# The experts' second layer by seven products of quarters, its input sums on GpSimd, the combination two experts behind

## The chip, the cores and the metric

The kernel runs on one core of one Trainium2 chip. The metric is the device time of one execution in microseconds (us), taken as the median over several executions. A core has five engines that work side by side, each through its own queue in order: TensorE (PE, with its weight loads shown apart as PEld), VectorE (DVE), ScalarE (ACT), GpSimd (POOL) and SyncE (SP, which here issues the DMAs).[...]

## The reference

Two stages run over 4096 tokens of 256 numbers (32 x 128 tokens), all in float32. Layer 0 is an attention block. Layer 1 is a windowed attention (24 tokens wide), followed by a mixture of eight experts, each with three dense layers:

```python
t = _to_tokens(x)                                    # after layer 0
t = t + _L1_attn_ref(_ln_t(t), K, temperature, bias) # window of 24 tokens
t = t + _L1_ffn_ref(_ln_t(t), ...)

def _L1_ffn_ref(x, Wr, br, W1, b1, ..., W2, b2, ..., Wo, bo):
    feat = jnp.mean(x, axis=0)
    w = jax.nn.softmax(feat @ Wr + br, axis=-1)      # weights of the 8 experts
    h = jnp.einsum('bfd,edh->bfeh', x, W1) + b1      # first layer,  256 -> 256
    h = jax.nn.relu(_bn(h, g1, be1, m1, v1))
    h = jnp.einsum('bfeh,ehk->bfek', h, W2) + b2     # second layer, 256 -> 256
    h = jax.nn.relu(_bn(h, g2, be2, m2, v2))
    y = jnp.einsum('bfeh,ehd->bfed', h, Wo) + bo     # third layer,  256 -> 256
    return jnp.einsum('bfed,fe->bfd', y, w)          # combination of the experts
```

The batch is one, so the mean over it changes nothing and every token has its own eight weights.

## The kernel before

The first 760 us or so are layer 0, which the change doesn't touch. The rest is one function in which windowed attention and experts run interleaved. Tokens lie in 32 tiles of 128, four tiles make a group (`TPB` = 4, so a block of `BLK` = 512 tokens), and there are eight groups (`NGRP`). For each group and each of the eight experts there is one work item, 64 in all.

The order on PE, ACT, DVE and POOL is written out by hand. Time is cut into slots. A slot first issues the attention steps that are due in it, those on other engines than PE first (the names in `POSTS`), then those on PE, and then one piece of expert work (`piece`). An engine takes its instructions exactly in this order. A work item has three pieces, a group 24 slots (`PERIOD` = 3 * 8). A slot number below is meant modulo 24, counted from the group's own first slot.

Attention steps of a group, with their slots: `project_out` (PE, 0 and 1), `residual` (DVE: an addition and the statistics of two tiles, 1 and 2; it also starts the load of a later pair, whose addition is on POOL), `root` (ACT, 3), `centre` (DVE, 4), `turn` and `turned` (PE and ACT, 5 to 7), `keys_tile` (POOL, 7), `project` and `projected` (PE and ACT, 8 to 10), `logits`, `rectified`, `weighed`, `windowed` (PE, DVE, ACT, DVE, 11 to 15), `gather` (PE, 15 and 17), `gathered` (DVE, 16 and 18: two tiles each time), `root` (ACT, 20). Then the experts' input is made: `expert_input` (DVE, 21), `expert_turn` (PE, 22), `expert_turned` (ACT, 23), `expert_sums` (DVE, 24), which writes four sums of quarters of the input. Then come the routing weights (`route` to `route_norm`, slots 26 to 31, that is 2 to 7 of the next group), `bias_sum` (POOL, in four slots from 32 on: the biases `bo` weighted and summed over the experts) and `biased` (DVE, 50, that is slot 2 two groups later: two additions).

Expert work. The first layer is a product of a 256 x 256 matrix with a 256 x 512 block. It is computed by Winograd's form of Strassen's method: both are cut into quarters, and seven products of a 128 x 128 quarter with 128 x 256 replace eight. `open_first` makes four of the products into two PSUM tiles `pa` and `pb`. DVE then reads them in four steps (lines 1825 to 1828, called the chain of four below) into `u` and `c`. `close_first` adds three more products on top, which is why its first two, into `pb`, must wait until the chain of four has read `pb`. DVE then makes two quarters more (line 1846), and ACT applies scale, shift and ReLU in three instructions (line 1856). The second layer (`layer`, line 1867) is plain: four products of 128 x 128 with 128 x 512, and two ACT instructions (line 1875). `combine` (lines 1892 and 1901) is the third layer: in each half four products of 256 columns and two DVE instructions that add the weighted result to `h1`.

The three pieces of work item k before are:

```python
part 0:  open_first(k + 1);       combine(k - 1, first half)
part 1:  combine(k - 1, second half);  close_first(k + 1)
part 2:  layer(k)
```

A float32 product shows in the profile as two matmul records. The two bank rings that matter are `ps_h` (four PSUM tiles: `pa`, `pb` and the second layer's two) and `ps_y` (two, for `combine`).

Of the kernel before, what the change touches and what calls it, by code (L numbers as in the profile page):

```python
# [9 lines left out]
F32 = mybir.dt.float32  # L10
AF = mybir.ActivationFunctionType
# [4 lines left out]
P = 128  # L16
# [807 lines left out]
def short(ctx: ExitStack, tc: tile.TileContext, ins: dict, out: bass.AP, flag):  # L824
# [538 lines left out]
    NRING = 12  # L1363
    with ExitStack() as ff:
# [23 lines left out]
        A = wf.tile([P, E, 7, P], F32, name="A")  # L1388
        W = {}
        for name in ("W2", "Wo"):  # L1390
            W[name] = wf.tile([P, E, 2, D], F32, name=f"{name}_sb")
        for e in range(E):
            w1 = ins["L1_ffn_W1"][e].rearrange("(c p) (m k) -> p c m k", p=P, k=P)
            a21 = fx.tile([P, P], F32, tag="a21", name=f"a21_{e}")
            nc.sync.dma_start(out=A[:, e, 0:2, :], in_=w1[:, :, 0, :])
            nc.sync.dma_start(out=a21, in_=w1[:, 0, 1, :])
            nc.sync.dma_start(out=A[:, e, 2, :], in_=w1[:, 1, 1, :])
            s = A[:, e]
            nc.gpsimd.tensor_tensor(s[:, 3], a21, s[:, 2], op=ALU.add)
            nc.gpsimd.tensor_tensor(s[:, 4], s[:, 3], s[:, 0], op=ALU.subtract)  # L1400
            nc.gpsimd.tensor_tensor(s[:, 5], s[:, 0], a21, op=ALU.subtract)
            nc.gpsimd.tensor_tensor(s[:, 6], s[:, 1], s[:, 4], op=ALU.subtract)
            for name in ("W2", "Wo"):
                nc.sync.dma_start(
                    out=W[name][:, e],
                    in_=ins[f"L1_ffn_{name}"][e].rearrange("(c p) h -> p c h", p=P),
                )
# [85 lines left out]
        def keys_tile(g):  # L1493

            kt = fx.tile([P, 2, 6 * P], F32, tag="kt", name=f"kt{g}")
            if g:
                old, at = kts[g - 1]
                base = (TPB * g + 1) * P - EDGE
                nc.gpsimd.tensor_copy(
                    kt[:, :, : P + EDGE], old[:, :, base - at : base - at + P + EDGE]  # L1500
                )
                kts[g] = kt, base
            else:
                kts[g] = kt, 0
# [14 lines left out]
        def projected(g, q):  # L1519
            kt, base = kts[g]  # L1520
            ps = banks.pop(("k", q)).rearrange("p (m k) -> p m k", m=2)
            nc.scalar.copy(kt[:, :, 2 * q * P - base : 2 * (q + 1) * P - base], ps)
# [6 lines left out]
        def logits(g, js, early=False):  # L1529
            kt, base = kts[g]  # L1530
# [22 lines left out]
        def rectified(js):  # L1553
            ps = banks.pop(("s", js[0])).rearrange("p (r k) -> p r k", r=2)
            pt = fx.tile([P, 2, WQ], F32, tag="pw", name=f"pw{js[0]}", bufs=4)
# [56 lines left out]
        def expert_input(b):  # L1612
            lo, hi = b * TPB, (b + 1) * TPB
            nc.vector.reciprocal(rstd2[:, lo:hi], rstd2[:, lo:hi])
            xf = fx.tile([P, TPB, D], F32, tag="xf", name=f"xf{b}", bufs=1)
            for r in range(TPB):
                normalise(lo + r, mean2, rstd2, xf[:, r, :])
            blk[b] = [xf]

        def expert_turn(b, early=False):  # L1620
            (xf,) = blk[b]
            pt = [bank(f"ptf{b}_{c}", early) for c in range(2)]
            for r in range(TPB):
                for c in range(2):
                    nc.tensor.transpose(
                        pt[c][:, r * P : (r + 1) * P], xf[:, r, c * P : (c + 1) * P], ident
                    )
            banks["x", b] = pt

        def expert_turned(b):  # L1630
            xfT = big_t[:, :, b * BLK : (b + 1) * BLK]
            for c, ps in enumerate(banks.pop(("x", b))):
                nc.scalar.copy(xfT[:, c, :], ps)
            blk[b] = [xfT]
# [3 lines left out]
        def expert_sums(b):  # L1638

            v = blk[b][0].rearrange("p c (n k) -> p c n k", n=2)  # L1640
            t = fx.tile([P, 4, HB], F32, tag="ts", name=f"ts{b}")
# [55 lines left out]
        def bias_sum(b, r):  # L1697

            w = blk[b][1]
            if r == 0:  # L1700
                blk[b].append(fx.tile([P, TPB, D], F32, tag="wb", name=f"wb{b}", bufs=1))
            out = blk[b][2][:, r, :]
            for k in range(2):
                t = fx.tile([P, E // 2, D], F32, tag="wbe", name=f"wbe{b}_{r}_{k}", bufs=1)
                es = slice(k * E // 2, (k + 1) * E // 2)
                nc.gpsimd.tensor_tensor(  # L1706
                    t, bo[:, es], w[:, r, es].unsqueeze(2).to_broadcast([P, E // 2, D]),
                    op=ALU.mult,
                )
                nc.gpsimd.tensor_tensor(t[:, :2], t[:, :2], t[:, 2:], op=ALU.add)  # L1710
                if k:
                    nc.gpsimd.tensor_tensor(t[:, 0], t[:, 0], t[:, 1], op=ALU.add)
                    nc.gpsimd.tensor_tensor(out, out, t[:, 0], op=ALU.add)
                else:
                    nc.gpsimd.tensor_tensor(out, t[:, 0], t[:, 1], op=ALU.add)
# [25 lines left out]
        def group(g):  # L1741
# [3 lines left out]
            js = list(range(TPB * g + 1 if g else 0, min(TPB * g + 5, NTILE)))  # L1745
            return qs, [js[k : k + 2] for k in range(0, len(js), 2)]

        def steps(g):
# [30 lines left out]
            put(21, expert_input, g)  # L1779
            put(22, expert_turn, g)  # L1780
            put(23, expert_turned, g)
            put(24, expert_sums, g)
# [255 lines left out]
```

## Time and profile before

| | |
|---|---|
| device time, median of 3 (lowest to highest) | 1552.93 us (1551.06 to 1554.34) |
| span of the profiled execution | 1551.5 us |
| layer 0 and the first group's attention | up to about 794 us |
| the interleaved stretch | 794 to 1551.5 us |
| one work item with no attention step in it | 9.91 us from open to open |
| the eight work items of a middle group | 95.5 us |
| DVE, ACT, POOL busy in the interleaved stretch (757.6 us) | 395.1, 263.8, 290.6 us |

The last three rows are read from the timeline: the starts of the first product of `open_first` (line 1819, `psa<-big_t,A`) are 9.91 us apart where no attention is left, as near the end, and 10.8 to 13.4 us apart where attention steps lie between. A timeline row gives start, busy time, engine, line, operation, output and inputs, and in brackets how long the engine had been idle and what ended it.

### The profile page before, as it was taken

The numbers are of one execution on the slowest core, as the hardware profiler recorded it, in microseconds if no ns is written. First come the engines' busy times: TensorE is split into PE (matmuls) and PEld (weight loads), VectorE is DVE, ScalarE is ACT, GpSimd is POOL, SyncE is SP. The second block draws the span as 40 slices with busy tenths as digits, with TensorE's granted clock in tenths as the row PEclk, the third lists the DMA queues.
The fourth block names the chain that finished last, engine by engine and source line by source line (L and its number), as shares of the span: only waits on it lengthen the run. The fifth ranks groups of instructions, "written<-read, shape, count | busy, mean of one in ns | idle before, by whom it ended". The sixth has DMA issues, their size and how long they took to land.

```text
span 1551.5 us, 22383 instructions
## 1 busy us (share of the span) xinstructions
PE 1514.8 (98%) x8932; PEld 818.6 (53%) x8932; DVE 995.1 (64%) x1461; ACT 823.1 (53%) x1077; POOL 359.6 (23%) x487
## 2 busy tenths in 40 slices
PE   7999999999999999999779999999999999999998
PEld 5663332222222222222357776777777777777775
DVE  5543567789888988989854555545455464555553
ACT  3225778788888888888433333333333334333332
POOL 0001110000000000000328053180622706226080
PEclk9999999999999999999999999999999999999999
DMA  4200000000000000000430000000000000000000
GB/s 119 62 1 14 18 9 9 9 8 8 8 9 2 8 9 1 8 3 7 131 94 0 7 21 1 28 1 7 21 1 28 0 1 14 1 14 1 14 1 16
DMA packets 32836, 27.71 MB, mean 18 GB/s; under 512 B 8098, under 2 KB 30616, under 8 KB 32724
## 3 DMA queue, kind: packets, MB, share of 16 engines
q1 hardware_dynamic: 31176, 24.73, 5.5%
q10 hardware_dynamic: 1548, 1.48, 0.4%
q8 instruction: 72, 1.18, 0.3%
q14 instruction: 40, 0.33, 0.1%
HBM read 21.75 MB, written 4.44 MB: 17 GB/s over the span
## 4 chain that ended last, share of the span: by engine, by line
PE 95%; DVE 2%; ACT 1%; DMA 0%; issue 0%; ACTq 0%; DVEq 0%
PE s L1234 20%; PE av L1271 17%; PE psy L1892 14%; PE psh L1867 14%; PE psb L1842 4%; PE psa L1819 3%; PE psb L1819 3%; PE z L1256 3%; PE psk L1080 2%; PE psk L1510 2%; PE psv L1106 2%; PE psq L1121 2%; PE psa L1842 2%; PE pso L1437 2%; PE pss L1535 1%; PE psa L1590 1%
## 5 line engine op out<-in xcount | busy, mean ns | idle before, releaser
L1243 ACT ACTIVATE pt<-s 128x1024 f32<-128x1024 f32 (+2 forms) x576 | 516.1, 951 | 113.8 <-PE s L1234 103.7
L1286 DVE TENSOR_TENSOR pt<-pt,pt 128x2048 f32<-128x2048 f32 x210 | 481.1, 2291 | 24.6 <-PE av L1271 4.6
L1234 PE MATMUL s<-QT,KT 32*128 32x512 f32 (+3 forms) x2304 | 338.5, 605 | 3.0 <-ACT pt L1243 2.2
L1271 PE MATMUL av<-pt,V 128*32 128x512 f32 (+3 forms) x2304 | 287.5, 571 | 0.0
L1892 PE MATMUL psy<-Wo_sb,h 128*128 128x256 f32 x1024 | 239.0, 381 | 0.9 <-ACT h L1875 0.9
L1856 ACT ACTIVATE h<-psa,bshift,bscale 128x256 f32<-128x256 f32 x64 | 36.1, 565 | 383.0 <-PE psa L1842 348.0
L1234 PEld LDWEIGHTS s<-QT,KT 32*128 32x128 f32 x2304 | 117.6, 183 | 227.6 <-issue 119.2
L1867 PE MATMUL psh<-h,W_sb 128*128 128x512 f32 x512 | 231.0, 594 | 0.0
L1892 PEld LDWEIGHTS psy<-Wo_sb,h 128*128 128x128 f32 x1024 | 192.6, 190 | 31.8 <-issue 4.8
L1901 DVE SCALAR_TENSOR_TENSOR h<-psy,w,h 128x256 f32<-128x256 f32 x256 | 111.9, 478 | 124.6 <-PE psy L1892 124.3
L1706 POOL TENSOR_TENSOR wbe<-bo,w 128x1024 f32<-128x1024 f32 x64 | 121.4, 1898 | 223.7 <-DVE w L1693 219.3
L1248 POOL MEMSET pt<- 64x256 f32 x64 | 20.0, 312 | 647.5 <-ACT pt L1243 570.3
L1271 PEld LDWEIGHTS av<-pt,V 128*32 128x32 f32 x2304 | 46.9, 108 | 195.6 <-issue 181.6
L1867 PEld LDWEIGHTS psh<-h,W_sb 128*128 128x128 f32 x512 | 95.9, 190 | 97.0 <-issue 94.5
L1875 ACT ACTIVATE h<-psh,bshift,bscale 128x512 f32<-128x512 f32 x128 | 98.0, 777 | 89.1 <-PE psh L1867 88.9
L1825 DVE COPY u<-psa 128x256 f32<-128x256 f32 x64 | 27.1, 423 | 166.2 <-PE psa L1819 166.2
L1856 ACT ACTIVATE h<-c,bshift,bscale 128x256 f32<-128x256 f32 (+1 forms) x128 | 82.8, 695 | 5.3 <-DVE c L1846 5.3
L1710 POOL TENSOR_TENSOR wbe<-wbe 128x512 f32<-128x512 f32 x64 | 82.6, 1291 | 5.0
L909 POOL TENSOR_TENSOR xr<-xr,outb 128x512 f32<-128x512 f32 x16 | 20.2, 1269 | 244.1 <-DMA xr<-in_x_dram 183.9
L1819 PE MATMUL psb<-ts,A 128*128 128x256 f32 x256 | 65.7, 379 | 0.0
L1256 PE MATMUL z<-pt,ones_m 128*32 128x512 f32 (+3 forms) x624 | 62.8, 475 | 2.2 <-DVE pt L1286 2.2
L1819 PEld LDWEIGHTS psb<-ts,A 128*128 128x128 f32 x256 | 48.6, 190 | 6.6
(179 smaller groups left out, 1417.2 us busy)
## 6 DMA issues: line engine op xcount, KB each, us to landing
xg<-in_x_dram SPq DMA_DIRECT2D x32, 128.0 KB
xr<-in_x_dram SPq DMA_DIRECT2D x16, 256.0 KB
out_dram<-h SPq DMA_DIRECT2D x16, 256.0 KB
rec<-rd SPq DMA_DIRECT2D x60, 64.0 KB
W_sb<-in_L_ffn_W_dram SPq DMA_DIRECT2D x8, 256.0 KB
Wo_sb<-in_L_ffn_Wo_dram SPq DMA_DIRECT2D x8, 256.0 KB
A<-in_L_ffn_W_dram SPq DMA_DIRECT2D x8, 128.0 KB
bo<-in_L_ffn_bo_dram SPq DMA_DIRECT2D x1, 896.0 KB
```

Source lines behind the costliest of these rows:

```text
L1234: nc.tensor.matmul(s[hh // 2][:, hh % 2, lo:], lhsT=KT[rows, g, i * P : (i + 1) * P], rhs=QT[rows, g, b * BLK + lo : (b + 1) * BLK], start ...
L1243: nc.scalar.activation(pt[:, 2 * hp : 2 * hp + 2, lo:], s[hp][:, :, lo:], AF.Exp, scale=SCALE)
L1256: nc.tensor.matmul(zs_ps[k][HD * hh : HD * (hh + 1), lo:], lhsT=ones_m[:, :HD], rhs=pt[:, hh, lo:], start=start, stop=stop,)
L1271: nc.tensor.matmul(avs[k][HD * hh : HD * (hh + 1), lo:], lhsT=V[:, i, (4 * g + hh) * HD : (4 * g + hh + 1) * HD], rhs=pt[:, hh, lo:], star ...
L1286: nc.vector.tensor_tensor(accs[k], accs[k], pt, op=ALU.add)
L1706: nc.gpsimd.tensor_tensor(t, bo[:, es], w[:, r, es].unsqueeze(2).to_broadcast([P, E // 2, D]), op=ALU.mult,)
L1819: nc.tensor.matmul(ps[:, cols], lhsT=lhsT, rhs=rhs, start=start, stop=False, skip_group_check=True,)
L1856: nc.scalar.activation(dst[:, m, cols], src, AF.Relu, bias=bshift[:, m, e : e + 1], scale=bscale[:, m, e : e + 1],)
L1867: nc.tensor.matmul(ps, lhsT=W[name][:, e, c, m * P : (m + 1) * P], rhs=src[:, c, :], start=(c == 0), stop=(c == 1),)
L1875: nc.scalar.activation(dst[:, m, :], ps, AF.Relu, bias=bshift[:, m, k : k + 1], scale=bscale[:, m, k : k + 1],)
L1892: nc.tensor.matmul(ps[:, k, :], lhsT=ht[:, c, r * P : (r + 1) * P], rhs=W["Wo"][:, e, c, :], start=(c == 0), stop=(c == 1),)
L1901: nc.vector.scalar_tensor_tensor(out=h1[q][:, k, :], in0=ps[:, k, :], scalar=w[:, r, e : e + 1], in1=h1[q][:, k, :], op0=ALU.mult, op1=ALU ...
```

## The change

The second layer is computed by seven products of quarters, as the first is: `open_layer` and `close_layer` serve both. The weights' quarters and their sums (`A`) now exist for both layers, so that POOL makes 64 instead of 32 sums when weights are loaded, and SP issues 56 instead of 40 weight loads. The four sums of quarters of the second layer's input are made on POOL in `close_first`, one of them in place. The second layer of an item is opened in part 1 and closed in part 2, and `combine` comes two items behind, its halves in parts 0 and 2. Closing starts with the product into `pa`, which was last. `expert_input`, `expert_turn` and `expert_turned` work in two halves, over slots 21 to 25, `expert_sums` moves to slot 25, and the first expert piece to slot 28 (was 27). `bias_sum` takes two experts at a time, in sixteen slots (32 to 47) instead of four. To make room, rings are smaller: `NRING` 8, `pw` 3, `ts` 1, one `kt` tile that is shifted in place, `wbe` of two experts; `c` has 2. The first group's logits are taken in pairs [0, 1], [2], [3, 4].

```diff
-    NRING = 12
+    NRING = 8
...
-        A = wf.tile([P, E, 7, P], F32, name="A")
-        W = {}
-        for name in ("W2", "Wo"):
-            W[name] = wf.tile([P, E, 2, D], F32, name=f"{name}_sb")
+        A = wf.tile([P, 2, E, 7, P], F32, name="A")
+        Wo = wf.tile([P, E, 2, D], F32, name="Wo_sb")
         for e in range(E):
-            w1 = ins["L1_ffn_W1"][e].rearrange("(c p) (m k) -> p c m k", p=P, k=P)
...
+            for l in range(2):
+                wl = ins[f"L1_ffn_W{l + 1}"][e].rearrange("(c p) (m k) -> p c m k", p=P, k=P)
+                a21 = fx.tile([P, P], F32, tag="a21", name=f"a21_{l}_{e}")
+                s = A[:, l, e]
+                nc.sync.dma_start(out=s[:, 0:2, :], in_=wl[:, :, 0, :])
+                nc.sync.dma_start(out=a21, in_=wl[:, 0, 1, :])
+                nc.sync.dma_start(out=s[:, 2, :], in_=wl[:, 1, 1, :])
+                nc.gpsimd.tensor_tensor(s[:, 3], a21, s[:, 2], op=ALU.add)
+                nc.gpsimd.tensor_tensor(s[:, 4], s[:, 3], s[:, 0], op=ALU.subtract)
+                nc.gpsimd.tensor_tensor(s[:, 5], s[:, 0], a21, op=ALU.subtract)
+                nc.gpsimd.tensor_tensor(s[:, 6], s[:, 1], s[:, 4], op=ALU.subtract)
+            nc.sync.dma_start(
+                out=Wo[:, e], in_=ins["L1_ffn_Wo"][e].rearrange("(c p) h -> p c h", p=P)
+            )
...
-        def expert_input(b):
...
+        def expert_input(b, k):
+            n0 = b * TPB + 2 * k
+            nc.vector.reciprocal(rstd2[:, n0 : n0 + 2], rstd2[:, n0 : n0 + 2])
+            xf = fx.tile([P, 2, D], F32, tag="xf", name=f"xf{b}_{k}", bufs=1)
+            for r in range(2):
+                normalise(n0 + r, mean2, rstd2, xf[:, r, :])
+            banks["xf"] = xf
+        def expert_turn(b, k, early=False):
+            xf = banks.pop("xf")
+            ps = bank(f"ptf{b}_{k}", early)
+            for r in range(2):
                 for c in range(2):
                     nc.tensor.transpose(
...
+                        ps[:, (2 * c + r) * P : (2 * c + r + 1) * P],
+                        xf[:, r, c * P : (c + 1) * P],
+                        ident,
+                    )
+            banks["x", b, k] = ps
+        def expert_turned(b, k):
+            lo = b * BLK + 2 * k * P
+            ps = banks.pop(("x", b, k)).rearrange("p (c k) -> p c k", c=2)
+            nc.scalar.copy(big_t[:, :, lo : lo + 2 * P], ps)
+            blk[b] = [big_t[:, :, b * BLK : (b + 1) * BLK]]
...
-        def bias_sum(b, r):
+        def bias_sum(b, r, k):
             w = blk[b][1]
-            if r == 0:
+            if r == 0 and k == 0:
                 blk[b].append(fx.tile([P, TPB, D], F32, tag="wb", name=f"wb{b}", bufs=1))
             out = blk[b][2][:, r, :]
-            for k in range(2):
-                t = fx.tile([P, E // 2, D], F32, tag="wbe", name=f"wbe{b}_{r}_{k}", bufs=1)
-                es = slice(k * E // 2, (k + 1) * E // 2)
-                nc.gpsimd.tensor_tensor(
-                    t, bo[:, es], w[:, r, es].unsqueeze(2).to_broadcast([P, E // 2, D]),
-                    op=ALU.mult,
-                )
-                nc.gpsimd.tensor_tensor(t[:, :2], t[:, :2], t[:, 2:], op=ALU.add)
-                if k:
-                    nc.gpsimd.tensor_tensor(t[:, 0], t[:, 0], t[:, 1], op=ALU.add)
-                    nc.gpsimd.tensor_tensor(out, out, t[:, 0], op=ALU.add)
-                else:
-                    nc.gpsimd.tensor_tensor(out, t[:, 0], t[:, 1], op=ALU.add)
+            t = fx.tile([P, 2, D], F32, tag="wbe", name=f"wbe{b}_{r}_{k}", bufs=1)
+            es = slice(2 * k, 2 * k + 2)
+            nc.gpsimd.tensor_tensor(
+                t, bo[:, es], w[:, r, es].unsqueeze(2).to_broadcast([P, 2, D]), op=ALU.mult
+            )
+            if k:
+                nc.gpsimd.tensor_tensor(out, out, t[:, 0], op=ALU.add)
+                nc.gpsimd.tensor_tensor(out, out, t[:, 1], op=ALU.add)
+            else:
+                nc.gpsimd.tensor_tensor(out, t[:, 0], t[:, 1], op=ALU.add)
...
-            put(21, expert_input, g)
-            put(22, expert_turn, g)
-            put(23, expert_turned, g)
-            put(24, expert_sums, g)
+            for k in range(2):
+                put(23 + 2 * k, expert_turned, g, k)
+                put(21 + 2 * k, expert_input, g, k)
+                put(22 + 2 * k, expert_turn, g, k)
+            put(25, expert_sums, g)
...
             for r in range(TPB):
-                put(32 + 4 * r, bias_sum, g, r)
+                for k in range(E // 2):
+                    put(32 + 4 * r + k, bias_sum, g, r, k)
             put(50, biased, g)
...
-        def open_first(b, e):
-            v = blk[b][0].rearrange("p c (n k) -> p c n k", n=2)
-            t, s = tsum[b], A[:, e]
-            pa = ps_h.tile([P, BLK], F32, tag="h", name=f"psa1_{b}_{e}")
-            pb = ps_h.tile([P, BLK], F32, tag="h", name=f"psb1_{b}_{e}")
+        def open_layer(l, v, t, b, e):
+            s = A[:, l, e]
+            pa = ps_h.tile([P, BLK], F32, tag="h", name=f"psa{l}_{b}_{e}")
+            pb = ps_h.tile([P, BLK], F32, tag="h", name=f"psb{l}_{b}_{e}")
             lo, hi = slice(0, HB), slice(HB, BLK)
             for ps, cols, lhsT, rhs, start in (
                 (pa, lo, s[:, 0], v[:, 0, 0], True),
-                (pa, hi, s[:, 4], t[:, 1], False),
-                (pb, hi, s[:, 5], t[:, 2], True),
-                (pb, lo, s[:, 3], t[:, 0], False),
+                (pa, hi, s[:, 4], t[1], False),
+                (pb, hi, s[:, 5], t[2], True),
+                (pb, lo, s[:, 3], t[0], False),
             ):
                 nc.tensor.matmul(
                     ps[:, cols], lhsT=lhsT, rhs=rhs, start=start, stop=False,
                     skip_group_check=True,
                 )
-            u = fh.tile([P, 2, HB], F32, tag="u", name=f"u{b}_{e}", bufs=1)
-            c = fh.tile([P, 3, HB], F32, tag="c", name=f"c{b}_{e}", bufs=1)
+            u = fh.tile([P, 2, HB], F32, tag="u", name=f"u{l}_{b}_{e}", bufs=1)
+            c = fh.tile([P, 3, HB], F32, tag="c", name=f"c{l}_{b}_{e}")
             nc.vector.tensor_copy(u[:, 1], pa[:, hi])
             nc.vector.tensor_tensor(u[:, 0], pa[:, lo], u[:, 1], op=ALU.add)
             nc.vector.tensor_tensor(u[:, 1], u[:, 0], pb[:, hi], op=ALU.add)
             nc.vector.tensor_tensor(c[:, 2], u[:, 1], pb[:, lo], op=ALU.add)
-            return pa, pb, u, c
-        def close_first(opened, b, e):
-            pa, pb, u, c = opened
-            v = blk[b][0].rearrange("p c (n k) -> p c n k", n=2)
-            t, s = tsum[b], A[:, e]
+            return v, t, pa, pb, u, c
+        def close_layer(opened, l, b, e):
+            v, t, pa, pb, u, c = opened
+            s = A[:, l, e]
             lo, hi = slice(0, HB), slice(HB, BLK)
             for ps, cols, lhsT, rhs in (
-                (pb, hi, s[:, 2], t[:, 3]),
+                (pa, lo, s[:, 1], v[:, 1, 0]),
+                (pb, hi, s[:, 2], t[3]),
                 (pb, lo, s[:, 6], v[:, 1, 1]),
-                (pa, lo, s[:, 1], v[:, 1, 0]),
             ):
                 nc.tensor.matmul(
                     ps[:, cols], lhsT=lhsT, rhs=rhs, start=False, stop=True,
...
                 c[:, 0:2], u[:, 0:1].to_broadcast([P, 2, HB]),
                 pb.rearrange("p (n k) -> p n k", n=2), op=ALU.add,
             )
-            dst = fh.tile([P, 2, BLK], F32, tag="h0", name=f"h0_{b}_{e}")
+            dst = fh.tile([P, 2, BLK], F32, tag=f"h{l}", name=f"h{l}_{b}_{e}")
+            k = l * E + e
             for m, cols, src in (
                 (0, lo, pa[:, lo]),
                 (0, hi, c[:, 0]),
...
             ):
                 nc.scalar.activation(
                     dst[:, m, cols], src, AF.Relu,
-                    bias=bshift[:, m, e : e + 1], scale=bscale[:, m, e : e + 1],
+                    bias=bshift[:, m, k : k + 1], scale=bscale[:, m, k : k + 1],
                 )
             return dst
-        def layer(src, name, l, b, e):
...
+        def quarters(x):
+            return x.rearrange("p c (n k) -> p c n k", n=2)
+        def open_first(b, e):
+            t = tsum[b]
+            return open_layer(0, quarters(blk[b][0]), [t[:, k] for k in range(4)], b, e)
+        def close_first(opened, b, e):
+            h = close_layer(opened, 0, b, e)
+            v = quarters(h)
+            t = fh.tile([P, 3, HB], F32, tag="th", name=f"th{b}_{e}")
+            nc.gpsimd.tensor_tensor(t[:, 0], v[:, 0, 1], v[:, 0, 0], op=ALU.subtract)
+            nc.gpsimd.tensor_tensor(t[:, 1], v[:, 1, 1], t[:, 0], op=ALU.subtract)
+            nc.gpsimd.tensor_tensor(v[:, 0, 1], v[:, 1, 1], v[:, 0, 1], op=ALU.subtract)
+            nc.gpsimd.tensor_tensor(t[:, 2], v[:, 1, 0], t[:, 1], op=ALU.subtract)
+            return v, [t[:, 0], t[:, 1], v[:, 0, 1], t[:, 2]]
...
             k, part = divmod(i - 1, 3)
-            ahead = k + 1 < len(work)
+            ahead, here, behind = k + 1 < len(work), k < len(work), k >= 2
             if part == 0:
                 if ahead:
-                    hs["open"] = open_first(*work[k + 1])
-                if k:
-                    combine(hs["t", k - 1], *work[k - 1], (0,))
+                    hs["1"] = open_first(*work[k + 1])
+                if behind:
+                    combine(hs["t", k - 2], *work[k - 2], (0,))
             elif part == 1:
-                if k:
-                    combine(hs.pop(("t", k - 1)), *work[k - 1], (1,))
                 if ahead:
-                    hs[k + 1] = close_first(hs.pop("open"), *work[k + 1])
-            elif k < len(work):
-                hs["t", k] = layer(hs.pop(k), "W2", 1, *work[k])
+                    hs[k + 1] = close_first(hs.pop("1"), *work[k + 1])
+                if here:
+                    hs["2"] = open_layer(1, *hs.pop(k), *work[k])
+            else:
+                if behind:
+                    combine(hs.pop(("t", k - 2)), *work[k - 2], (1,))
+                if here:
+                    hs["t", k] = close_layer(hs.pop("2"), 1, *work[k])
...
-        n_pieces = 3 + 3 * len(work)
-        START = 27
+        n_pieces = 1 + 3 * (len(work) + 2)
+        START = 28
```

## The prediction

> **What bounds the kernel now.** I read the busy table, then PE's share of the chain of waits, then busy time by stretch for one middle group of eight items (columns: PE, PEld, DVE, ACT, POOL).
>
> ```profile
> PE 1514.8 (98%) x8932; PEld 818.6 (53%) x8932; DVE 995.1 (64%) x1461; ACT 823.1 (53%) x1077; POOL 359.6 (23%) x487
> ...
> PE 95%; DVE 2%; ACT 1%; DMA 0%; issue 0%; ACTq 0%; DVEq 0%
> ...
> 1071.30:1166.90 95.60, 95.60 (x411) 70.48 (x410) 51.04 (x125) 33.72 (x54) 37.37 (x31) 1.00 0.04 12
> ```
>
> PE never rests, at full granted clock; the others work about half the time or less. Whether "busy" means full speed is told by the spacing of starts, in the timeline of one item:
>
> ```profile
> 1529.63 3.60 PE L1867 MATMUL psh<-h,W_sb 128*128 128x512 f32 x8
> 1533.06 0.59 PE L1892 MATMUL psy<-Wo_sb,h 128*128 128x256 f32 x2
> ...
> 1126.93 1.03 PE L1819 MATMUL psb<-ts,A 128*128 128x256 f32 x4
> 1127.13 0.42 DVE L1825 COPY u<-psa 128x256 f32<-128x256 f32 x1 [3.68 <-PE psa L1819]
> 1127.80 2.54 PE L1892 MATMUL psy<-Wo_sb,h 128*128 128x256 f32 x11
> 1128.65 0.42 DVE L1828 TENSOR_TENSOR c<-u,psb 128x256 f32<-128x256 f32 x1
> ...
> 803.10 0.48 PE L1842 MATMUL psb<-ts,A 128*128 128x256 f32 x1 [1.39 <-DVE c L1828]
> ```
>
> Eight records of 512 columns take 3.43 us (1529.63 to 1533.06), so 0.43 each. Opening starts at 1126.07 and `combine` at 1127.80: eight records of 256 columns in 1.73, 0.216 each. The records follow without gaps: PE is the bound, and fewer columns are less time. The last line is the one wait that can hurt: `pb` can't be closed before the chain of four has read it. It cost 1.39 us at the start, where no `combine` lay between; else that hides it.
>
> [...]
>
> ```profile
> 898.52 1.27 POOL L909 TENSOR_TENSOR xr<-xr,outb 128x512 f32<-128x512 f32 x1 [10.95 <-PE psh L1867]
> ...
> 898.59 2.45 DVE L1467 TENSOR_SCALAR xl<-h,mean,rstd 128x256 f32<-128x256 f32 x4
> ...
> 941.13 1.89 POOL L1706 TENSOR_TENSOR wbe<-bo,w 128x1024 f32<-128x1024 f32 x1
> ...
> 941.87 1.57 DVE L1575 TENSOR_TENSOR pw<-pw,window 128x384 f32<-128x384 f32 x1
> ```
>
> Four `xl` instructions normally take 1.38 us together; here 2.45, the first ending only after POOL's. The window product ends at 943.44, 0.42 after POOL's instruction (943.02). The chain of four reads PSUM and keeps 0.42 an instruction under POOL.
>
> **The change, part by part,** against the profiled span, 1551.5 us (1.4 below the runs' median).
>
> *PE, removed:* per item 8 x 0.43 = 3.43 us become 14 x 0.216 = 3.02. 0.41 x 64 = 26 us saved, all on the path. No other PE work is added.
>
> *DVE and ACT, added:* a second chain of four (1127.13 to 1129.07, 1.94) and a second `c` (0.69): 2.6 x 64 = 168 us. With 395 that is 563 of about 750: no bound on average. ACT has 1.94 for 1.55 an item: 264 + 25 us, hidden beside PE.
>
> *POOL:* four sums of 128x256, 0.73 and 0.08 to the next: 3.2 us an item. `bias_sum` in pieces: the trace has no weighting of 512 columns; between 0.73 (an addition of 256) and 1.29 (one of 512); I take 1.05, from 1.90 for 1024 and the additions' slope. With two additions a piece is 2.75 (1.95 for the first of four), 40.8 a group. In slots 8 to 23 that is 40.8 + 5.3 x 3.2 = 58 us, and PE has 62 there. Sums have three slots until they are needed, so this fits, but in the last group, without attention work, PE has 50.5: 7.5 short, less 4 of lead: +3.5 us.
>
> *The wait that moves in.* Closing comes half a `combine` after opening, not a whole one. Let opening end at 0. The chain ends at 1.27 (1129.07 less 1127.80). PE does half a `combine` (1.73), then the `pa` product (0.43), and wants `pb` at 2.16. Slack: 0.85 us. DVE is in order, and attention's DVE steps stand ahead of the chain. The built program's order shows which:
>
> Slots 1 and 2. Clock zero: end of the second layer's opening in slot 0. PE: `project_out` 1.73, half `combine` 3.46, closing 4.75, `route` 5.33, opening 7.06, half `combine` 8.79, `pa` 9.22. DVE: chain 1.27, `expert_sums` (1.55) 2.8, `residual` (1.85) 4.7, two `combine` additions (0.88) 5.55, `c` 6.25, `biased` (1.21) 7.45, `residual` 9.3, chain (1.92) 11.2. PE stands 2.0 us. In the kernel before slot 2 carried part 1, with no chain due.
>
> [...]`expert_sums` has two SBUF inputs; it and POOL's second-layer sums are released by ACT at the same moment, right after the ReLUs. Taking turns, they end near 4.45 instead of 2.8: +1.6. The first `residual` frees a buffer whose load lands 2.86 later (1074.34 to 1077.20), and POOL's 1.27 us addition then falls at about 8.0, on `biased` (7.9 to 9.1): between 0 and 1.3, I take 0.65. Together 2.0 + 1.6 + 0.65 = 4.3 us, at six boundaries: 26 us[...].
>
> Slot 18. Clock zero: end of half `combine` in slot 17. DVE: additions 1.08, `gathered` (2.6) 3.7, `c` 4.4, chain 6.3. PE: closing 1.29, opening 3.02, half `combine` 4.75, `pa` 5.18: 1.15 us, seven times: 8 us.
>
> Slots 4 and 5: `centre`'s four, interleaved with POOL's sums, pass the slack by 0 to 1.0: 0.5 x 7 = 3.5. Slots 14, 21 and 23 (`windowed`, `expert_input` under `bias_sum`): 0 to 0.6, 0.3 x 7 = 2.
>
> *Start and end.* Three more closings have no `combine` before them, 0.95 each (1.39 less the `pa` product): 2.8. POOL makes 32 more weight sums at 0.46 beside the first group's attention, SP issues 16 more loads at 0.48 ahead of `bo` and `xr`, and expert work starts a slot later: 0 to 5, I take 2. At the end the wait of `combine` for its own ReLU goes (0.44 idle at 1534 and again at 1542): -0.9.
>
> *At nothing:* smaller rings (`xl` 8 tiles: one is overwritten after its reader in the group before; `pw` and `kt` likewise); the two halves of `expert_input` (same totals); `combine` an item later (one more live tile in a ring of two, freed by PE just before).
>
> Sum: -26 + 26 + 8 + 3.5 + 2 + 3.5 + 2.8 + 2 - 0.9 = +20.9 us. 1552.9 + 20.9 = 1573.8.
>
> **The rivals.** A measurement here can tell about 0.2%, 3 us, from no change.
>
> *A, my forecast:* the saved columns are spent standing before `pb` at slots 2 and 18, about 1574 us, own range 1560 to 1590. For it: order and durations are known. Against it: slack is short in both directions; a releaser half a microsecond earlier, six times over, is 3 us.
>
> *B, PE stays the bound* and DVE's surplus is absorbed (faster). Mechanism: in slot 2 DVE enters the attention steps ahead of PE, because slots with PE steps (0, 1, 8 to 17) give it time to catch up. Price: -26 + 5 at the start, 1532; with one of the two stalls left, up to 1547. It decides if DVE reaches the chain less than 0.85 us after it could. For it: DVE is at 75% on average, and before its steps were hidden. Against: slot 2 alone stacks 3.06 us of DVE on 1.2 of slack and of `route`.
>
> *C, queue waits without the lock:* the boundary costs 2.0, slots 4 and 14 to 23 nothing: -26 + 12 + 8 + 3.5 + 3.6 = +1, 1554. Against: the 2.45 us row.
>
> *D, POOL becomes the bound in slots 8 to 23:* it has 58 of 62 us. [...]another 8% on its own instructions is 4 us a group, seven times: 1574 + 28 = 1602. Against: POOL's additions now differ little, 0.73 free and 0.92 at worst under a lock.
>
> **How the numbers follow.** A 0.52, B 0.23, C 0.12, D 0.13. The predicted time is A's. Faster: B and a fifth of C, 0.25. Within 0.2%: two fifths of C, 0.06 with what A holds near zero. The rest, 0.69, slower. A range of 1535 to 1598 leaves out the lower half of B and two thirds of D, about 0.2; A alone is 1560 to 1590.
>
> **What would show it.** Right: PE idle before the closing line's `psb`, ended by DVE's `c` of the chain, 2 us or more at each group boundary and 1 us once more per group; `expert_sums` rows well over 0.42 where POOL runs; items without attention steps at 9.5 us from open to open (9.91 before). Wrong: such idle under 10 us in all (B), or PE idle at opening, ended by POOL's `th` (D), or 9.9 us for a bare item, which would say the seven products save nothing.

## The result, and the profile after

| | before | after |
|---|---|---|
| device time, median (lowest to highest) | 1553.63 us (1551.06 to 1555.18) | 1562.24 us (1559.86 to 1563.09) |
| ratio, 95% interval | | 1.0055 (1.0036 to 1.0073) |
| span of the profiled execution | 1551.5 us | 1560.8 us |
| first product of the expert stretch starts at | 799.72 us | 802.36 us |
| from there to the end | 751.8 us | 758.4 us |
| four full groups in the middle, eight items each | 95.5, 95.5, 95.5, 95.5 us | 95.9, 99.0, 98.7, 95.9 us |

The change made the kernel slower by 0.55%, where 1.35% was forecast. The page of the changed kernel, its busy table and the first line of its chain of waits:

```profile
PE 1504.1 (96%) x9316; PEld 892.4 (57%) x9316; DVE 1156.6 (74%) x1789; ACT 853.1 (55%) x1141; POOL 580.7 (37%) x903
...
PE 86%; DVE 10%; issue 1%; DMA 1%; ACT 1%; ACTq 0%; DVEq 0%; POOL 0%; POOLq 0%
```

PE's share of the chain fell from 95% to 86%, and DVE's rose from 2% to 10%: PE is no longer the bound all the way. Busy time in the stretch of the middle group (PE, PEld, DVE, ACT, POOL, then PE's granted clock):

```profile
1071.30:1166.90 95.60, 92.14 (x444) 77.66 (x443) 69.25 (x160) 35.76 (x60) 60.09 (x76) 0.98 0.04 12
```

DVE went from 51 to 69 us of 95.6 and POOL from 37 to 60; PE now rests 3.5 us here, and its granted clock was 0.98 instead of 1.00. Who kept PE waiting is in the list of waits of the stretch from 790 us on (waiter and line, then what ended the wait: total idle us, times, longest):

```profile
PE psa L1839 <- DVE u L1824: 11.6, 15, 3.1
PE psb L1839 <- DVE c L1826: 5.6, 15, 0.8
PE pso L1435 <- ACT big_t L1629: 4.3, 5, 0.9
```

Lines 1823 to 1826 are the chain of four, line 1839 the closing. Closing's first product waits already for the chain's second step (`pa` must have been read), which the prediction overlooked; its second, into `pb`, waits for the fourth. The third row, `project_out` waiting for ACT's copy in `expert_turned` (line 1629), is in no step of the prediction.

The saving is there. The starts of the first product of `open_first` near the end, where no attention step is left (timeline of the changed kernel):

```profile
1493.05 0.59 PE L1817 MATMUL psa<-big_t,A 128*128 128x256 f32 x2
...
1502.55 0.59 PE L1817 MATMUL psa<-big_t,A 128*128 128x256 f32 x2
```

They are 9.50 us apart, 0.41 less than before: 64 x 0.41 = 26 us saved, as forecast. What gave it back is seen at one ordinary boundary between groups:

```profile
1178.81 0.56 ACT L1629 COPY big_t<-ptf 128x512 f32<-128x512 f32 x1
...
1179.42 1.99 PE L1435 MATMUL pso<-woT,big_t 128*128 128x256 f32 x8 [0.86 <-ACT big_t L1629]
...
1180.12 0.83 DVE L1639 TENSOR_TENSOR ts<-big_t,ts 128x256 f32<-128x256 f32 x1
...
1180.88 0.94 DVE L1640 TENSOR_TENSOR ts<-big_t 128x256 f32<-128x256 f32 x1
...
1185.24 1.29 DVE L1713 TENSOR_TENSOR h<-h,wb 128x512 f32<-128x512 f32 x2
...
1189.15 0.70 PE L1839 MATMUL psa<-big_t,A 128*128 128x256 f32 x2 [0.49 <-DVE u L1824]
...
1190.13 0.70 PE L1839 MATMUL psb<-ts,A 128*128 128x256 f32 x2 [0.28 <-DVE c L1826]
```

First `project_out` stands still for 0.86 us. Two of the four steps of `expert_sums` take 0.83 and 0.94 where 0.42 was usual before, and the two of POOL's sums beside them 0.90 instead of 0.73. This is what the recorded texts call the lock, as far as the traces show it: instructions of the two engines that take longer side by side. What makes them do so isn't shown. Then closing waits 0.49 and 0.28. Measured from start to start, over the usual 0.22 us, this is 1.03 + 0.65 + 0.44 = 2.1 us. Two boundaries are worse; here the one near 1090 us:

```profile
1086.56 2.36 DVE L1713 TENSOR_TENSOR h<-h,wb 128x512 f32<-128x512 f32 x2
...
1086.95 1.42 POOL L909 TENSOR_TENSOR xr<-xr,outb 128x512 f32<-128x512 f32 x1 [4.09 <-DMA xr<-in_x_dram]
...
1091.55 0.70 PE L1839 MATMUL psa<-big_t,A 128*128 128x256 f32 x2 [1.56 <-DVE u L1824]
...
1092.53 1.19 PE L1839 MATMUL psb<-ts,A 128*128 128x256 f32 x2 [0.28 <-DVE c L1826]
1093.51 1.06 PE L1839 MATMUL psb<-big_t,A 128*128 128x256 f32 x2
1094.37 1.06 PE L1817 MATMUL psa<-h,A 128*128 128x256 f32 x2
```

`biased` runs into POOL's addition of `xr`, the collision that the prediction named, and takes 2.36 us instead of 1.29: PE waits 1.08 us longer. Then pairs of records start 0.86 apart instead of 0.43: the granted clock was 0.50 for 3.41 us, which costs 1.7 more. The stop after slot 18's two gathers recurs in every group; timeline of the changed kernel:

```profile
1155.55 1.89 PE L1886 MATMUL psy<-Wo_sb,h 128*128 128x256 f32 x8
1157.74 0.70 PE L1839 MATMUL psa<-h,A 128*128 128x256 f32 x2 [0.30 <-DVE u L1824]
1158.88 0.67 PE L1839 MATMUL psb<-th,A 128*128 128x256 f32 x2 [0.44 <-DVE c L1826]
```

The ledger of PE's extra time between starts in the stretch, by place, beside the prediction's terms. The places named are sums of pauses over 0.2 us in the two profiled executions:

| | forecast, us | measured, us |
|---|---|---|
| columns saved | -26 | -26.2 |
| closing at six boundaries | 26 | 9.8 (three of 1.1, three of 2.2) |
| `project_out` at five boundaries | none | 5.1 |
| half clock after two of the boundaries | none | 3.4 |
| after slot 18's gathers | 8 | 7.8 |
| slots 4, 5, 14 to 23, POOL in the last group | 9 | none (in the last group 0.7 once, ended by DVE) |
| start, first group | 4.8 | 2.6 later, 2.5 more in waits, 1.7 half clock: 6.8 |
| end | -0.9 | -1.2 |
| the rest, single pauses of up to 0.5, not assigned | | 3.8 |
| sum, profiled spans | +20.9 | +9.3 |

### The profile page after: what moved, and what is told of

Same layout as the page of the kernel before. It is cut to its first block, busy times and chain, and to the rows that moved or that the text cites. A ratio compares the mean times of both kernels' runs of the same rounds, so it can differ in the third digit from the quotient of the medians.

```text
span 1560.8 us, 24419 instructions
## 1 busy us (share of the span) xinstructions
PE 1504.1 (96%) x9316; PEld 892.4 (57%) x9316; DVE 1156.6 (74%) x1789; ACT 853.1 (55%) x1141; POOL 580.7 (37%) x903
## 3 DMA queue, kind: packets, MB, share of 16 engines
q10 hardware_dynamic: 1548, 1.48, 0.4%
## 4 chain that ended last, share of the span: by engine, by line
PE 86%; DVE 10%; issue 1%; DMA 1%; ACT 1%; ACTq 0%; DVEq 0%; POOL 0%; POOLq 0%
PE s L1234 20%; PE av L1271 17%; PE psy L1886 12%; PE psb L1839 7%; PE psa L1817 6%; PE psb L1817 6%; PE z L1256 3%; PE psa L1839 3%; PE psk L1080 2%; PE psk L1503 2%; PE psv L1106 2%; PE psq L1121 2%; PE pss L1528 1%; DVE st L1458 1%; PE psa L1576 1%
## 5 line engine op out<-in xcount | busy, mean ns | idle before, releaser
L1854 ACT ACTIVATE h<-c,bshift,bscale 128x256 f32<-128x256 f32 (+1 forms) x256 | 167.1, 699 | 177.4 <-DVE c L1843 177.4
L1854 ACT ACTIVATE h<-psa,bshift,bscale 128x256 f32<-128x256 f32 x128 | 72.3, 565 | 267.0 <-PE psa L1839 243.3
L1886 PEld LDWEIGHTS psy<-Wo_sb,h 128*128 128x128 f32 x1024 | 193.5, 190 | 26.2
L1843 DVE TENSOR_TENSOR c<-u,psb 128x512 f32<-128x512 f32 x128 | 87.5, 683 | 79.1 <-PE psb L1839 79.1
L1701 POOL TENSOR_TENSOR wbe<-bo,w 128x512 f32<-128x512 f32 x128 | 133.3, 1041 | 6.3
L1872 POOL TENSOR_TENSOR th<-h 128x256 f32<-128x256 f32 x64 | 46.7, 730 | 182.1 <-ACT h L1854 182.0
L1823 DVE COPY u<-psa 128x256 f32<-128x256 f32 x128 | 54.0, 422 | 46.2 <-PE psa L1817 44.6
L1705 POOL TENSOR_TENSOR wb<-wb,wbe 128x256 f32<-128x256 f32 x96 | 72.5, 755 | 7.5
L1706 POOL TENSOR_TENSOR wb<-wb,wbe 128x256 f32<-128x256 f32 x96 | 70.9, 738 | 7.5
L1825 DVE TENSOR_TENSOR u<-u,psb 128x256 f32<-128x256 f32 x128 | 53.9, 421 | 13.9 <-DVE u L1824 0.5
L1826 DVE TENSOR_TENSOR c<-u,psb 128x256 f32<-128x256 f32 x128 | 53.9, 421 | 11.9 <-DVE u L1825 0.9
```

The source lines that it names most:

```text
L1701: nc.gpsimd.tensor_tensor(t, bo[:, es], w[:, r, es].unsqueeze(2).to_broadcast([P, 2, D]), op=ALU.mult)
L1843: nc.vector.tensor_tensor(c[:, 0:2], u[:, 0:1].to_broadcast([P, 2, HB]), pb.rearrange("p (n k) -> p n k", n=2), op=ALU.add,)
L1854: nc.scalar.activation(dst[:, m, cols], src, AF.Relu, bias=bshift[:, m, k : k + 1], scale=bscale[:, m, k : k + 1],)
L1886: nc.tensor.matmul(ps[:, k, :], lhsT=ht[:, c, r * P : (r + 1) * P], rhs=Wo[:, e, c, :], start=(c == 0), stop=(c == 1),)
```

## The experiments

Times are medians; beside each stands the ratio to the kernel before with its 95% interval. "Stretch" is from the first expert product to the end of the profiled execution (758.4 us in the changed kernel); it leaves out that layer 0 ends up to 5 us earlier or later from run to run.

**The plain second layer back, all else kept.** POOL's four sums for each item go with it, as do the sums of the second layer's weights.

```diff
-                    hs["2"] = open_layer(1, *hs.pop(k), *work[k])
...
-                    hs["t", k] = close_layer(hs.pop("2"), 1, *work[k])
+                    hs["t", k] = layer(hs.pop(k), *work[k])
```

> The changed kernel with the plain second layer put back (four products of 512 columns, no sums on GpSimd); combination two behind, halved input, small rings and the later start stay. Queue theory (the seven products save 26 us, and DVE's order gives some 35 back: 12 at the group boundaries, 7 at slot 18's gathered, 6 at a new wait of project_out, 7 at the start): the boundary wait of the first layer, the project_out wait and the start remain, so 1562 to 1568 us, bare items at 9.91 us again. Rival 'the seven products save nothing on PE': 1545 or less, since only their costs would go.

1576.36 us, ratio 1.0152 (1.0126 to 1.0178): a miss, 8 us above the upper expectation. The boundary's closing waits, expected to stay, are gone (outside the first group none is left), but `project_out` waits three times as long; its row in the waits of this kernel, and the place in its timeline:

```profile
PE pso L1439 <- ACT big_t L1633: 12.9, 5, 2.6
```

```profile
1185.95 1.99 PE L1439 MATMUL pso<-woT,big_t 128*128 128x256 f32 x8 [2.58 <-ACT big_t L1633]
```

The second layer's opening, 1.73 us of PE work just ahead of `project_out`, is gone, so `project_out` arrives 1.73 earlier and waits 1.72 longer. The granted clock was 0.989 on average, as in the changed kernel. The copy that it waits for is one of the side changes, not of the seven products: with as many columns as the kernel before, the side changes alone make the stretch 23 us longer (774.8 against 751.8). With them already made, the products are worth 14 us (1576.4 to 1562.2; 16 in the stretch).

**The bias addition four slots later.**

```diff
-            put(50, biased, g)
+            put(54, biased, g)
```

> The changed kernel with the bias addition moved from slot 50 (slot 2, ahead of the chain of four) to slot 54 (slot 6, where DVE has no other attention step). Queue theory: the boundary wait of about 1.1 us goes six times, and with it the two long ones of 1.8 us that were followed by half the TensorE clock (2.8 us each in all): 1562 - 12 = 1550 us, no half clock after the start. Lock theory[...]: expert_sums stays locked, only the collision of the bias addition with the xr addition goes, two groups at 2.8: 1556.

1549.38 us, 0.9986 (0.9979 to 0.9993), as expected; stretch 745.2. Its waits:

```profile
PE psa L1839 <- DVE u L1824: 6.0, 10, 3.2
...
PE psb L1839 <- DVE c L1826: 3.8, 10, 0.4
```

At five of six boundaries closing no longer waits, and the granted clock was 0.992 on average instead of 0.989. What is left is 1.2 us at the last one. The ledger gives 8.6 us for these waits and 3.4 for the half clock after two of them, 12.0; the medians are 12.9 apart, the stretches 13.2. One slot number is worth more than the whole loss.

**The second tile of each pair gathered one slot later** (16, 17, 18 and 19 instead of two in 16 and two in 18).

```diff
-                put(16 + k, gathered, i0 + k + 1)
+                put(17 + k, gathered, i0 + k + 1)
```

> The changed kernel with gathered spread one tile a slot (16, 17, 18, 19) instead of two in slots 16 and 18. Queue theory: 1.3 us of DVE work in slot 18 fits the slack, the wait of about 1.07 us before the closing products in slot 19 goes seven times: 1562 - 7 = 1555 us. Rival: the wait only moves to slots 17 or 19, where the other tile now stands: 1561.

1560.34 us, 1.0063 (1.0046 to 1.008). The rival was right: the wait moved. Waits of this kernel:

```profile
PE psa L1839 <- DVE u L1824: 9.4, 8, 3.0
PE psa L1576 <- DVE h L1598: 7.2, 7, 1.0
```

The second row is new: `gather` of slot 17 (line 1576) now waits for the first pair's bank, which `gathered` (line 1598) frees only in slot 17. From start to start it is 1.20 us, seven times, about as much as was taken away in slot 19. By the ratios this kernel can't be told from the changed one (1.0063 and 1.0055). Its stretch is 3.7 us shorter, 754.7: the stops at the six boundaries are the same, but the granted clock was 0.992 on average, against 0.989.

**The biases left out** (`bias_sum` and `biased`, so the output lacks `bo`'s share).

```diff
-                for k in range(E // 2):
-                    put(32 + 4 * r + k, bias_sum, g, r, k)
-            put(50, biased, g)
+                pass
```

> The changed kernel without the bias sums on GpSimd and without the bias addition on DVE (the weighted biases are left out of the output). Queue theory: as moving the bias addition away, and GpSimd's 40.8 us a group cost nothing, since they hold up only expert_input and windowed, which have slack: 1549 us. Lock theory: DVE's locked instructions under the bias sums[...] go as well, 1542 or less.

1547.81 us, 0.9974 (0.9966 to 0.9982). Removing 41 us of POOL work a group, which stood beside most of DVE's attention steps, is worth 1.6 us more than moving one DVE step. So it was `biased`'s place in DVE's queue, and what DVE's steps lose beside `bias_sum` (a step of `expert_input` took 0.83 in the median and up to 1.20 in the changed kernel, 0.41 before) costs next to nothing.

**`biased` in slot 54 and only the second pair of gathers parted** (18 and 19; 16 keeps both of the first).

```diff
-                put(16 + k, gathered, i0 + k + 1)
+                put(16 + 3 * k // 2, gathered, i0 + k + 1)
```

> The bias addition in slot 54 as in the run before, and of gathered only the second pair split: two tiles in slot 16, one each in slots 18 and 19, so that the banks of gather in slot 17 are free as before. Queue theory: the wait of about 1.07 us in slot 19 goes seven times and none takes its place, 1549.4 - 7 = 1542.5 us. Rival: the second tile in slot 19 delays the closing there as much as two in slot 18 did: 1549.

1543.8 us, 0.9944 (0.9926 to 0.9962), stretch 736.4. The stretch is 8.8 shorter than with `biased` alone (the medians are 5.6 apart; the expert stretch began 5.6 us later in this profiled run). The pauses after slot 18 are gone. Waits:

```profile
PE psa L1839 <- DVE u L1824: 4.0, 3, 3.2
...
PE psb L1839 <- DVE c L1826: 1.1, 4, 0.4
```

**Biases out, and the experts' turned input in a tile of its own** instead of a part of `big_t`, to see what `project_out` waits for.

```diff
+            if k == 0:
+                blk[b] = [fx.tile([P, 2, BLK], F32, tag="xfT", name=f"xfT{b}")]
...
-            nc.scalar.copy(big_t[:, :, lo : lo + 2 * P], ps)
+            nc.scalar.copy(blk[b][0][:, :, lo : lo + 2 * P], ps)
```

> Without the biases (their sums, the addition and the tile bo are left out of the computation, to free the room), and the experts' input in a tile of its own with two buffers instead of in big_t. To be compared with the run without biases, 1547.8 us. If the wait of project_out in slot 1 (0.86 us idle, 1.03 between starts, five times) comes only from both living in big_t, it goes: 1547.8 - 5 = 1542.5 us. If it hides another wait (its PSUM bank, freed by residual), 1547.

1548.22 us, 0.998 (0.9971 to 0.9989): no gain over 1547.81. The wait is unchanged under the new name:

```profile
PE pso L1432 <- ACT xfT L1628: 4.3, 5, 0.9
```

So it isn't the shared tile. What is left is the PSUM bank: `expert_turn`'s two halves and `project_out`'s two halves draw from one ring of two (`ps_x`), and the third and fourth users need the banks of the first two back. This is an inference so far; the last two experiments test it.

**The second layer's sums on DVE**, with `biased` in slot 54 (one execution).

```diff
-            nc.gpsimd.tensor_tensor(t[:, 0], v[:, 0, 1], v[:, 0, 0], op=ALU.subtract)
+            nc.vector.tensor_tensor(t[:, 0], v[:, 0, 1], v[:, 0, 0], op=ALU.subtract)
```

(and the other three likewise)

> The bias addition in slot 54, and the second layer's input sums on DVE instead of GpSimd. DVE would then wait in its queue for the ReLUs that the sums read, ahead of the chain of four: per item about 1.5 us of waiting and 1.6 us of sums against 0.85 us of slack, so 2 us lost on 64 items, 1549 + 130 = 1680 us. If only DVE's average load counts (about 85%), 1560 us.

1722.57 us in one execution. Worse than either expectation:

```profile
PE psa L1839 <- DVE u L1824: 92.2, 66, 4.2
PE psb L1839 <- DVE c L1826: 17.5, 61, 0.6
```

PE's waits for the chain of four stand at nearly every item now. The two rows are 110 us, against 10 in the version with POOL, which took 173 us less. Its granted clock was 0.967 on average over 1720.8 us, against 0.992 over 1546.9; (1 - 0.967) x 1720.8 less (1 - 0.992) x 1546.9, some 44 us, is an estimate of what that cost. The rest was not taken apart.

**The second layer's sums left out** (the products read quarters of the input in their place, so the values differ).

```diff
-            return v, [t[:, 0], t[:, 1], v[:, 0, 1], t[:, 2]]
+            return v, [v[:, 0, 1], v[:, 1, 1], v[:, 0, 1], v[:, 1, 0]]
```

> The changed kernel with the second layer's input sums left out (plain quarters stand in their place, so the values are others); bias sums and the bias addition stay in slots 32 to 47 and 50. Lock theory: expert_sums runs in 1.55 instead of 2.5 us, the boundary wait of 1.1 us shrinks to about 0.1 six times, and the two half clocks go: 1562 - 6 - 6 = 1550 us. If DVE's plain amount of work sets the wait and the lock is hidden: 1560.

1559.07 us, 1.0056 (1.0039 to 1.0072): by the ratios no faster than the changed kernel (1.0055); the stretch is 6.0 us shorter, 752.4. The two long steps of `expert_sums` at the same boundary:

```profile
1175.57 0.42 DVE L1639 TENSOR_TENSOR ts<-big_t,ts 128x256 f32<-128x256 f32 x1
1175.91 0.42 DVE L1640 TENSOR_TENSOR ts<-big_t 128x256 f32<-128x256 f32 x1
```

POOL's sums were what made the steps longer: without them all four take 0.42 instead of 0.50, 0.83, 0.94 and 0.41. Closing at the six boundaries still waits 7.9 us in all (9.8 with the sums), and the granted clock was 0.992 on average instead of 0.989. The total hides how much the longer steps are worth, since POOL's `xr` addition now meets `biased` at three boundaries instead of two. The last boundary has no collision in either run, and no wait of `project_out`; the changed kernel first, then this one:

```profile
1379.23 0.70 PE L1839 MATMUL psa<-big_t,A 128*128 128x256 f32 x2 [1.58 <-DVE u L1824]
```

```profile
1373.87 0.70 PE L1839 MATMUL psa<-big_t,A 128*128 128x256 f32 x2 [0.53 <-DVE u L1824]
```

The product after it waits 0.28 in both. From start to start closing loses 2.19 with POOL's sums and 1.14 without: here all of the 1.0 us by which `expert_sums` is longer reaches PE. At boundaries with a wait of `project_out` and no collision it is 1.09 with the sums (three of them) and 0.93 without (two). There `project_out` has delayed PE by 1.0 us already, and without the sums DVE waits for PE's products, near 1276 us for 0.66 us in all:

```profile
1276.32 0.69 DVE L1843 TENSOR_TENSOR c<-u,psb 128x512 f32<-128x512 f32 x1 [0.42 <-PE psb L1839]
```

So the longer steps are a part of what the boundary costs. Where `project_out` waits, that wait seems to cover most of it; no run removes both to show it. Moving `biased` (1.3 us of DVE) took away the closing waits of five boundaries with POOL's sums in place.

**`project_out`'s second half in slot 2**, with the two moves above (`biased` in 55); `root`, `centre`, `turn` and the routing softmax one slot later with it.

```diff
-                put(k + 1, residual, q)
-                put(k, project_out, q)
+                put(2 * k + 1, residual, q)
+                put(2 * k, project_out, q)
```

> The bias addition in slot 55, the second pair of gathers copied one tile a slot (18 and 19), and project_out's second half one slot later (2 instead of 1), with what follows it (residual 1 and 3, root 4, centre 5, turn 6 and 7, turned 7 and 8, the routing softmax 30 to 32). If project_out stood still because its PSUM bank still held the second half of the experts' turned input, which ACT copies in slot 1: its wait (4.3 us of idle, five times 1.03 from start to start) goes, slots 5 and 7 are a little fuller (0 to 2 us in all): against 1543.8 us without that move, 1537 to 1541 us. If something else held it (the copy itself coming late, or PE merely losing there what it would lose at the boundary's closing): the idle stays near 4 us under project_out or reappears at the closing, 1543 to 1546 us.

1545.22 us, 0.9953 (0.9936 to 0.9969), stretch 739.1: within the rival's range. But the reason that ended the wait was another:

```profile
PE pso L1435 <- DVE h L1447: 6.1, 6, 2.3
```

ACT's copy is no longer in it; a `residual` is (five waits of 0.75 in the stretch; the sixth, of 2.3, is before it). In slot 2 `route` now came before `project_out`, took the free bank, and the second half was given the bank of the first. That is the ring again, one user further on, and it made a prediction that could be tried:

**The same, with `route`, its copy and its turning one slot later.**

```diff
-            put(26, route, g)
-            put(27, copy_route, g)
-            put(28, turn_route, g)
+            put(27, route, g)
+            put(28, copy_route, g)
+            put(29, turn_route, g)
```

> As the run before (project_out's second half in slot 2), with the routing product, its copy and its turning one slot later (27, 28, 29 instead of 26, 27, 28). In the run before, project_out's wait for ACT's copy was gone, but it stood still 4.05 us for a residual of slot 1 instead: route had taken the bank between the two halves, so the second half got the bank of the first. If a bank of the ring of two is what holds project_out, its order is now turn, turn, first half, second half, route, each freed a slot or more before: the wait of project_out goes (under 0.5 us in all), 1545.2 less 4: 1541 us. If it is something else: the idle stays near 4 us, 1545 us.

1537.02 us, 0.9893 (0.9874 to 0.9912), stretch 733.0. PE's waits of more than 1 us in all:

```profile
PE ptf L1619 <- DVE xf L1465: 4.8, 2, 4.3
PE psr L1650 <- DVE h L1447: 2.8, 1, 2.8
PE psa L1839 <- DVE u L1824: 2.7, 3, 1.7
PE psb L1839 <- DVE c L1826: 1.2, 5, 0.3
```

`project_out` isn't in the list. Of the 8.2 us against the run before, 4.6 are its wait (five of 0.92 from start to start); in the profiled runs the stretch is 6.1 shorter and begins 4.7 us earlier, the latter nothing that the edit touches in the code. The waiter moved as the order of the ring's users says, twice, and the wait went with the order that frees each bank in time: the ring of two is the cause. This version is 1.07% faster than the kernel before: 18.8 us less in the stretch, of the 26.2 that the products save.

## Why the prediction was right or wrong

*Right: the direction, the saving, the kind of wait.* PE at 0.216 us a record gave 9.50 us a bare item (9.5 forecast). The waits sit where the built order put them, at the boundary and after slot 18, and moving one DVE step past each removed them (at the boundary five of six). Slot 18 was priced at 8 us and measured 7.8; POOL's weighting of 512 columns at 1.05 and measured 1.04.

*Wrong: the boundary's size, 26 us forecast, 9.8 measured at closing.* This is the step that failed; even with `project_out`'s wait (5.1), which took part of its place, and the half clock (3.4) it is 18.3. All three parts of "2.0 + 1.6 + 0.65" were mis-sized.

- The queue: it stands alone at the last boundary of the run without the second layer's sums, and cost 1.14. That boundary has one `residual` and one half of `project_out` less, and the prediction's own sums give 1.9 for it. DVE ended the chain 8.9 us after the clock zero, where they say 9.35, and PE wanted `pb` at 7.7, where they say 7.5.
- POOL's sums beside DVE's, "Taking turns, they end near 4.45 instead of 2.8: +1.6": this was the author's estimate. They did lengthen `expert_sums`, from 1.68 (four of 0.42) to 2.68 (0.50, 0.83, 0.94, 0.41). That is 1.0, not 1.6, and the prediction added the whole of it to PE's wait at each boundary: it reached PE whole where nothing else had delayed PE, and with 0.16 at boundaries where `project_out` had.
- The collision, "between 0 and 1.3, I take 0.65": it isn't a mean of 0.65, but 1.08 at two boundaries of six and none at the others, and behind these two the granted clock was 0.50 for 3.41 us, which no term had.

*Wrong: "at nothing: the two halves of `expert_input` (same totals)".* The totals are the same, but the second half's copy moved from slot 23 to 25, which is slot 1, where `project_out` needs the bank. 5.1 us, the largest single thing that was missed. The prediction looked at rings of SBUF tiles and not at the order in which a PSUM ring is taken.

*Wrong: slots 4 and 5, 14 to 23, and POOL's shortage in the last group, 9 us.* No such wait of PE is seen there. How DVE made up for the interleaving with POOL there was not looked into.

*The rivals.* C, "queue waits without the lock", summed to 1554 (its 3.6 for start and end should be 3.9). It was right that most of what POOL's sums add to DVE's steps is hidden at the ordinary boundaries, with a chance of 0.12 against 0.52 for A. But it gives no reason, and what seems to hide it is the wait for the bank, which it lacks. That 1554 with the 5.1 of the bank and the 3.4 of the half clock comes to the time measured is luck: its 12 for the boundary was 9.8 with POOL's sums, and its 3.5 for POOL did not occur. B fell for this order of steps; with the steps moved, its 1532 to 1547 is where the kernel stands. D fell: no product of PE is listed as waiting for POOL's sums. That the time still lies inside the range of 1535 to 1598 is luck too: prices too high for the boundary and for slots that cost nothing, against a bank and a half clock that were not seen.

## What to carry to other kernels

Work saved on the bound engine is kept only if nothing in order stands ahead of what the shorter stretch now waits for. For each place where the distance between a producer and its reader shrinks, list what stands ahead of the producer in its queue in every slot, and move these steps before anything else is judged: one number was worth 13 us here. Do the same for each ring of buffers: write down who takes which bank in which order, since splitting one user in two shifts every later one. An operation that takes longer beside another engine's is not yet a wait: a price for it enters the sum only where its end is what the next engine waits for. And one wait can cover another, so judge such a price at a place where nothing else waits.

## What the runs showed of the hardware

A short stop of PE was followed by a lower granted clock at some places and not at others. In the changed kernel the stretches at a granted clock of 0.50 between the first expert product and 1548 us start at 809.29, 993.61 and 1092.60 us, each 3.41 us long; the starts lie 54 and 29 times 3.413 us apart. Divided into steps of that length from 812.71 us on, and back from there, the trace has PE busy for 1.65, 1.57 and 1.56 us in the step before each of the three. No other step from there to 1548 us has PE busy for less than 1.83 us. That one, from 1375.91 on, holds the first stop of the closing near 1379 (1.58 us idle) and not the second (0.28), which lies in the next step; near 1090 and 993 both, 1.56 and 0.28, lie in one step. The granted clock after 1379.32 was 1.00. In the kernel before, divided likewise from 797.31 us on, the least busy step, from 800.72 on, has 2.02 us, and the granted clock after it was 1.00.

So two stops of the same length were followed by 3.41 us at a granted clock of 0.50 in two places, where they fell into one step, and not in a third, where they fell into two. These are readings of two traces; no run tried by itself what decides it.
